# An LSTM layer with a residual: the bias by an accumulating DMA, and other amounts of work in the last 43 steps

## The chip, the cores and the metric

The kernel runs on one core of a Trainium2 chip. The metric is the device time of one execution in microseconds (us); the lower, the better. A core has five engines that work beside one another, each through its own list of instructions in order: TensorE (PE in the profile; PEld is its weight load), VectorE (DVE), ScalarE (ACT), GpSimd (POOL) and SyncE (SP). Here SP does nothing but issue DMAs; sixteen DMA engines move the data. TensorE writes into PSUM, eight banks of 128 partitions x 512 fp32 columns; everything else lives in SBUF or in DRAM.

## The reference

An LSTM layer with 512 time steps, a batch of 32 and 512 hidden units, all in fp32; its output is added to its input.

```python
xW = jnp.einsum('ntd,dg->ntg', x, Wx) + b          # (32, 512, 2048)
def step(carry, xw_t):
    prev_h, prev_c = carry
    a = xw_t + prev_h @ Wh                         # Wh: 512 x 2048
    i = jax.nn.sigmoid(a[:, :Hd]);  f = jax.nn.sigmoid(a[:, Hd:2 * Hd])
    o = jax.nn.sigmoid(a[:, 2 * Hd:3 * Hd]);  g = jnp.tanh(a[:, 3 * Hd:])
    next_c = f * prev_c + i * g
    next_h = o * jnp.tanh(next_c)
    return ((next_h, next_c), next_h)
return x + hs                                      # hs: all next_h; h0 = cond_1024, c0 = 0
```

Two matrix products of the same size are in it. The recurrent one, prev_h @ Wh, has to be done step by step. The input product x @ Wx can be done ahead for many time steps at once, and the kernel does it with a fast matrix multiplication (sums of blocks of x, sums of blocks of Wx, fewer products, and then sums of the products).

## The kernel before, in words

**Steps.** The loop `for k in range(T)` at the end of the kernel writes out 512 steps. In step k TensorE adds the recurrent product (`h_part`, L755: 16 matmuls of 384 columns and 16 of 128) onto PSUM banks that already hold xW + b for this step. They were seeded by ScalarE copies of the tile `xw[k]`: `seed_first` (L740, 384 columns, in step k-2) and `seed_last` (L746, 128 columns, in step k-1). The cell (`cell`, L792 to L800) is a chain of ScalarE and VectorE operations that ends in a transpose, L800, whose output `ht` is what the next step's matmuls wait for. `put_step` (L853) then adds the residual on Pool, and every second step SP stores two steps of output (L856) and loads two steps of residual (`load_residual`, L223).

**Windows.** Step k also carries window v = k + 4 of the input product. Steps 0 to 19 serve the head (48 time steps); from window START = 24 on come fourteen superblocks of 32 time steps each. A superblock has R = 26 products, begun in 26 of its 32 windows, and each product is seven groups of four 256-column matmuls (`product`, L465), spread over five windows by `products`. ScalarE and VectorE empty the banks in `evacuate`. VectorE's sums are kept in a list `due`, each with a window by which it has to be done and a cost in columns; `run_due(v, room)` runs what is due now, and ahead of time as much as `room` columns allow, each sum at its columns plus FIXED = 160. A window's allowance is ROOM = 4300 columns (HEAD_ROOM = 5000 in the head). At its start `evacuate` runs sums up to FIRST_SUMS = 1200 columns. The sums are L400 (blocks of x), L428 to L431 (the four inner sums, 128 x 128), L628 (half of a sum of products, 512 columns), L644 (a whole one, 1024 columns), L499 and L506 (within a product). Finished sums go to DRAM by `store` (L528, four DMAs).

**The bias.** In step k SP loads the tile `xw[k+3]`, 128 x 512 fp32, from DRAM (`load_xw`, L714), and Pool adds the bias to `xw[k+2]` in place (`add_bias`, L717). `bias_sb` is a constant 128 x 512 tile in SBUF. There are four `xw` buffers. 488 time steps take this way: the first 8 and the last 16 (the tail, t = 496 to 511) do not. Their plain products (`direct`, L670) are added to the bias by VectorE on the way from PSUM (`keep_direct`, L686).

**The order on SP.** SP issues in program order: in a step the residual load, the xw load, the stores, then `fetch` (L916: the factors wa of the product two windows on; L920: wb of this window's), then the output store.

**Half steps.** The last window of superblock products begins at LAST = 470. From step HALVES = 469 on, the cell is done in two halves of the hidden units (`h_halves`, L769, with 256-column matmuls; `cell_halves`, L814 to L840, chain ends L830), so that the next step's matmuls can begin on the first half of `ht`. In these 43 steps the free room on TensorE holds the tail's plain products: 16 time steps x NJ = 4 pieces (t, q), each of four 512-column matmuls. `tail_products(v)` takes one piece in the first window and two in each one after, until all 64 are done; that is in step 501.

Of the kernel before, what the change touches and what calls it, by code (L numbers as in the profile page):

```python
# [9 lines left out]
F32 = mybir.dt.float32  # L10
# [4 lines left out]
P = 128  # L15
B = 32
T = 512
NJ = 4
G = 4
# [3 lines left out]
C = 256  # L23
# [15 lines left out]
TAIL = 2 * ROW  # L39
NSB = (T - HEAD - TAIL) // PER  # L40
END = HEAD + NSB * PER
# [5 lines left out]
ROOM = 4300  # L47
FIRST_SUMS = 1200
BETWEEN = 1300
HEAD_ROOM = 5000  # L50
COPIED = (23, 24, 25)
SLACK = [3, 3, 5, 8]
AHEAD = 5
# [88 lines left out]
def windows_of(k):  # L142

    return [k + 4]


START = windows_of(HEAD - LEAD)[0]
# [4 lines left out]
def begin(n):  # L152

    half, at = divmod(n, R // 2)
    return PER // 2 * half + at + (at >= 5) + (at >= 9)
# [7 lines left out]
LAST = START + PER * (NSB - 1) + begin(R - 1)  # L163
HALVES = LAST + 3 - 4
# [7 lines left out]
def kernel(  # L172
# [9 lines left out]
    nc = tc.nc  # L182
# [5 lines left out]
    upool = ctx.enter_context(tc.tile_pool(name="upool", bufs=1))  # L188
# [13 lines left out]
    bias_sb = const.tile([P, G * P], F32, name="bias_sb")  # L202
# [3 lines left out]
    raw = [raw_sb[:, i] for i in range(8)]  # L206
    tt_ = [const.tile([P, 4, C], F32, name=f"t_{i}") for i in range(8)]
    rows, xw, stored = {}, {}, {}
# [11 lines left out]
    def load_residual(t):  # L220
        m = xr[t] = xr[t + 1] = opool.tile([P, 2, NJ, B], F32, name=f"xr_{t}", tag="xr")
        i, a = divmod(t, ROW)
        nc.sync.dma_start(  # L223
            out=m.rearrange("p t q b -> p (t q b)"),
            in_=x[i][:, a * P : (a + 2) * P],
        )
# [24 lines left out]
    def t_sums(i):  # L251
        w, t = raw[i], tt_[i]
        return [
            lambda: nc.vector.tensor_sub(t[:, 0::3], w[:, 1::2], w[:, 0:2]),
            lambda: nc.vector.tensor_sub(t[:, 1], w[:, 3], t[:, 0]),
            lambda: nc.vector.tensor_sub(t[:, 2], w[:, 2], t[:, 1]),
        ]
# [290 lines left out]
    for i, (_, a, b) in enumerate(C_OPS):  # L548
        n = ready[R + i]
        uses[a] += 1  # L550
        uses[b] += 1
        for v, other in ((a, b), (b, a)):
            if v < R and (v != n or other == v or n in COPIED):
                copied.add(v)
# [6 lines left out]
    for v in range(len(ready) - 1, R - 1, -1):  # L561
        n = ready[v]
        if (n in C_OPS[v - R][1:] and n not in COPIED) or any(ready[u] == n and (u in at_half) for u in users[v]):
            at_half.add(v)
# [5 lines left out]
    for v in range(len(ready) - 1, R - 1, -1):  # L570
        n = ready[v]
# [90 lines left out]
    def flat(bank):  # L662
        return bank if len(bank.shape) == 2 else bank.rearrange("p n c -> p (n c)")

    def direct(t, bank, qs=range(4)):
        i, a = divmod(t, ROW)
        for q in qs:
            k, e = divmod(q, 2)
            for j in range(NJ):
                nc.tensor.matmul(  # L670
                    flat(bank)[j * B : (j + 1) * B],
                    rows[i][:, a, q],
                    raw[NJ * k + j][:, 2 * e : 2 * e + 2].rearrange("p n c -> p (n c)"),
                    start=q == 0,
                    stop=True,
                    skip_group_check=True,
                )

    def keep_direct(t, bank, room=None):
        if room is not None:  # L680
            xw[t] = room
        elif t < 4:
            xw[t] = upool.tile([P, G * P], F32, name=f"xw_{t}", tag="xw", bufs=4)
        else:
            xw[t] = node_free[t - 4].rearrange("p t e b -> p (t e b)")
        nc.vector.tensor_add(xw[t], flat(bank), bias_sb)  # L686

    pieces = [(t, q) for t in range(END, T) for q in range(NJ)]
    whole = []
    tail_banks = [p5, accs[1 - LAST % 2], accs[LAST % 2], *pps]  # L690

    def tail_room():
        if not node_free:
            f = free.pop(0)
            node_free.extend(f[:, e].rearrange("p (t e b) -> p t e b", t=ROW, e=2) for e in range(2))
        return node_free.pop(0).rearrange("p t e b -> p (t e b)")

    def tail_products(v):
        if v < LAST + 3:
            return  # L700
        for t in whole:
            keep_direct(t, tail_banks[(t - END) % 6], tail_room())
        whole.clear()
        room = 1 if v <= LAST + 3 else 2
        for t, q in pieces[:room]:
            direct(t, tail_banks[(t - END) % 6], (q,))
            if q == NJ - 1:
                whole.append(t)
        del pieces[:room]

    def load_xw(t):
        xw[t] = upool.tile([P, G * P], F32, name=f"xw_{t}", tag="xw", bufs=4)
        i, a = divmod(t, ROW)
        nc.sync.dma_start(out=xw[t], in_=stored[i][a])  # L714

    def add_bias(t):
        nc.gpsimd.tensor_add(xw[t], xw[t], bias_sb)  # L717

# [15 lines left out]
    def seed_first(t):  # L736
        if t == HALVES:
            seed_half(t, 0)
        elif t < HALVES:
            nc.scalar.copy(gates[t % 2][:, 0:IFG], xw[t][:, 0:IFG])  # L740
# [131 lines left out]
    def prepare(v):  # L872

        job = jobs.get(v)
        ops = []
        if job is None or job.w >= START:
            return ops
        i, j = job.kind
        for k in range(2):
            if (i, k) not in head_sums:  # L880
                if (i, 0) not in head_sums:
                    both = spool.tile([P, 2, 4, 4, B], F32, name=f"s_h{i}", tag="sums", bufs=2)
                head_sums[i, k], more = inner_sums(block(raw_block(i, k)), both[:, k])
                ops += more
        job.factors = lambda s: [
            (left(block(raw_block(i, k)), s, head_sums[i, k]), raw_factor(NJ * k + j, s)) for k in range(2)
        ]
        job.finish = finish_unit(job, i, j)
        job.release = lambda: None
        return ops  # L890
# [45 lines left out]
    with tc.manual_schedule():  # L936
        warm = work.tile([P, G, P], F32, name="warm", tag="s")
        nc.scalar.activation(warm[:, 0], c_init, AF.Sigmoid)
        for m in range(3 * NJ):
            nc.tensor.matmul(  # L940
                pps[2][m % NJ * B : (m % NJ + 1) * B].rearrange("p n c -> p (n c)"),
                c_init[:, 0:B],
                c_init.unsqueeze(1).to_broadcast([P, 4, P]),
                start=True,
                stop=True,
            )
        nc.vector.transpose(
            bias_sb.rearrange("p (m l) -> p m l", l=B),
            bias_t.unsqueeze(2).to_broadcast([P, G * NJ, B]),
        )  # L950
        firsts = [gates[0], gates[1], pps[0], pps[1]]
        for q in range(4):
            for t in range(4):
                direct(t, firsts[t], (q,))
        for i in range(6):
            for op in t_sums(i):
                op()
        for op in prepare(0):
            op()
        products(0)  # L960
        for t in range(4):
            keep_direct(t, firsts[t])
        for i in range(6, 8):
            for op in t_sums(i):
                op()
        push_factors()
        for v, t in enumerate(range(4, ROW), 1):
            direct(t, gates[t % 2])
            for op in prepare(v):
                op()  # L970
            if v < 4:
                evacuate(v, 0)
            run_due(0, 2400)
            keep_direct(t, gates[t % 2])
            if v < 4:
                products(v)
                fetch(v)
        seed_first(0)
        seed_last(0)
        seed_first(1)  # L980

        for k in range(T):
            if k % 2 == 0 and k + 2 < T:
                load_residual(k + 2)
            if 2 * 4 - 3 <= k and k + 3 < END:
                load_xw(k + 3)
            (h_part if k < HALVES else h_halves)(k)
            if 2 * 4 - 2 <= k and k + 2 < END:
                add_bias(k + 2)
            for m, v in enumerate(windows_of(k)):  # L990
                if v == START + 4:
                    assert len(due) == 0 or due[0][0] >= START
                    head_done()
                announce(v)
                room = ROOM if v >= START - 4 else HEAD_ROOM
                run_due(v, room - evacuate(v, room))
                products(v)
                tail_products(v)
                fetch(v)
                if k == T - 2:  # L1000
                    x_last()
                if m == 0:
                    (cell if k < HALVES else cell_halves)(k)
                    seed_first(k + 2)
                    seed_last(k + 1)
                for op in prepare(v + 1):
                    op()
        assert not due
# [51 lines left out]
```

## Time and profile before

| | |
|---|---|
| median of 3 runs | 3136.37 us (3133.24 to 3139.02) |
| the profiled execution | 3136.89 us, span 3135.0 us, granted clock 1.00 |
| TensorE busy | 3101.0 us, 99% |
| VectorE busy | 2421.7 us, 77% |
| ScalarE busy | 1697.0 us, 54% |
| Pool busy | 1030.9 us, 33% |
| DMA queue of SP | 683.39 MB, 67.3% of 16 engines' span |

The span is the time from the first to the last instruction. A row of the timeline reads: start, duration (us), engine, line of the kernel, operation, output <- inputs, partitions x elements, number of instructions merged into the row, and in brackets how long the engine had been idle before and what released it. Ends of matmuls are modelled; their starts are the safer number. A row of a group of instructions reads: line, engine, operation, tiles, count | total busy us, mean ns of one | idle time of the engine before them and what ended most of it. A row of a DMA group ends in the size of one and the median time from issue to landing.

### The profile page before, as it was taken

To read this page: it belongs to the slowest core of one execution; us is meant where nothing else is said; L and a number is where in the kernel's file an instruction comes from. 1 tells how busy PE (TensorE), PEld (TensorE's weight loads), DVE (VectorE), ACT (ScalarE), POOL (GpSimd) and SP (SyncE) were. 2 spreads that over 40 slices of the span, in tenths; PEclk is the share of its full clock that TensorE was granted. 3 is DMA by queue.
4 is the path that set the end of the run, shared out by engine and by line. 5 is a ranking of instruction groups with operands and counts; after the bars stand their busy time and mean duration, and the time that the engine had idled before them with its cause. 6 is when DMAs were issued, how large, how long until landed. Compare 5 with 4: busy or idle time off the path is not lost.

```text
span 3135.0 us, 133350 instructions
## 1 busy us (share of the span) xinstructions
PE 3101.0 (99%) x56184; PEld 1986.8 (63%) x56184; DVE 2421.7 (77%) x6337; ACT 1697.0 (54%) x5186; POOL 1030.9 (33%) x1001
## 2 busy tenths in 40 slices
PE   9999999999999999999999999999999999999997
PEld 4665666666666666666666666666666666666565
DVE  6637787887888878788787887878888788887544
ACT  2445555555555555555555555555555555555444
POOL 0223333333333333333333333333333333333320
PEclk9999999999999999999999999999999999999999
DMA  8746776767768676676777767777686776867420
GB/s 293 246 147 212 239 241 202 265 214 248 228 207 263 219 253 212 225 253 216 251 229 230 243 223 246 224 240 241 203 269 210 243 234 208 265 215 234 142 66 25
DMA packets 341287, 691.93 MB, mean 221 GB/s; under 512 B 44752, under 2 KB 113360, under 8 KB 340176
## 3 DMA queue, kind: packets, MB, share of 16 engines
q1 hardware_dynamic: 340544, 683.39, 67.3%
q8 instruction: 442, 7.24, 1.0%
q14 instruction: 157, 1.29, 0.1%
q10 hardware_dynamic: 144, 0.01, 0.0%
HBM read 501.56 MB, written 181.67 MB: 218 GB/s over the span
## 4 chain that ended last, share of the span: by engine, by line
PE 76%; DVE 18%; ACT 3%; issue 2%; DMA 1%; DVEq 0%; SPq 0%; ACTq 0%
PE gates L755 39%; PE pp L465 13%; PE acc L465 13%; PE p L465 4%; PE gates L769 4%; DVE t L644 2%; DVE s L430 1%; DVE t L628 1%; DVE raw_sb L644 1%; DVE c L797 1%; ACT ig L798 1%; DVE ht L800 1%; DVE fc L799 1%; PE pp L670 1%; DVE s L428 1%
## 5 line engine op out<-in xcount | busy, mean ns | idle before, releaser
L755 PE MATMUL gates<-wh_sb,ht 128*32 128x384 f32 (+1 forms) x29952 | 1714.5, 380 | 12.0 <-DVE ht L800 9.5
L755 PEld LDWEIGHTS gates<-wh_sb,ht 128*32 128x32 f32 x29952 | 1026.0, 110 | 718.5 <-issue 600.8
L853 POOL TENSOR_TENSOR oc<-xr,ht 128x128 f32<-128x128 f32 x509 | 406.0, 798 | 1997.3 <-DVE ht L800 1794.7
L717 POOL TENSOR_TENSOR xw<-xw,bias_sb 128x512 f32<-128x512 f32 x488 | 640.5, 1313 | 89.9 <-DMA xw<-xw 53.4
L792 ACT ACTIVATE s<-gates 128x256 f32<-128x256 f32 x469 | 180.2, 384 | 570.0 <-PE gates L755 570.0
L465 PE MATMUL pp<-wb,nodes 128*32 128x256 f32 x3808 | 306.1, 379 | 0.0
L799 DVE TENSOR_TENSOR fc<-s,ig 128x128 f32<-128x128 f32 x469 | 138.3, 295 | 176.3 <-ACT ig L798 176.3
L504 ACT COPY pp<-pu 128x512 f32<-128x512 f32 x384 | 231.7, 603 | 60.2 <-DVE t L628 22.1
L795 DVE TENSOR_TENSOR fc<-s,c 128x128 f32<-128x128 f32 x468 | 140.8, 301 | 143.8 <-ACT s L792 141.8
L798 ACT ACTIVATE ig<-c 128x128 f32<-128x128 f32 x469 | 145.3, 310 | 165.5 <-DVE c L797 145.4
L740 ACT COPY gates<-xw 128x384 f32<-128x384 f32 x465 | 219.8, 473 | 4.8 <-DVE nodes L686 3.0
L794 ACT ACTIVATE s<-gates 128x128 f32<-128x128 f32 x469 | 130.1, 277 | 170.2 <-PE gates L755 170.2
L506 DVE TENSOR_TENSOR pp<-acc,p 128x256 f32<-128x256 f32 x384 | 162.8, 424 | 69.3 <-ACT pp L505 69.3
L465 PE MATMUL acc<-wb,s 128*32 128x256 f32 x2576 | 207.1, 380 | 1.0
L465 PE MATMUL p<-wa,s 128*32 128x256 f32 x2576 | 206.9, 379 | 0.0
L465 PE MATMUL pp<-wb,s 128*32 128x256 f32 x2576 | 206.8, 379 | 0.0
L465 PE MATMUL acc<-wa,s 128*32 128x256 f32 x2576 | 206.7, 380 | 0.0
L499 DVE TENSOR_TENSOR pu<-acc,p 128x256 f32<-128x256 f32 x384 | 159.4, 415 | 35.1 <-ACT p L496 21.9
L800 DVE STREAM_TRANSPOSE ht<-fc 128x128 f32<-128x128 f32 x469 | 146.0, 311 | 50.1 <-DVE fc L799 1.4
L505 ACT COPY pp<-acc 128x256 f32<-128x256 f32 x384 | 139.0, 362 | 77.3 <-DVE t L628 28.4
L769 PE MATMUL gates<-wh_sb,ht 128*32 128x256 f32 x2752 | 157.5, 379 | 14.7 <-DVE fc L820 14.7
L496 ACT COPY p<-p 128x256 f32<-128x256 f32 x384 | 146.4, 381 | 28.0 <-PE p L465 25.8
(218 smaller groups left out, 4637.2 us busy)
## 6 DMA issues: line engine op xcount, KB each, us to landing
wb<-keep_b SPq DMA_DIRECT2D x322, 512.0 KB, 5.5
xw<-xw SPq DMA_DIRECT2D x488, 256.0 KB, 4.2
wa<-keep_a SPq DMA_DIRECT2D x322, 384.0 KB, 4.4
xw<-t SPq DMA_DIRECT2D x348, 128.0 KB, 3.6
xw<-raw_sb SPq DMA_DIRECT2D x280, 128.0 KB, 3.1
xr<-in_x_dram SPq DMA_DIRECT2D x256, 128.0 KB, 3.1
out_dram<-oc SPq DMA_DIRECT2D x255, 128.0 KB, 2.6
row<-in_x_dram SPq DMA_DIRECT2D x63, 512.0 KB, 6.7
```

Of the source, the lines that this page charges most:

```text
L465: nc.tensor.matmul(dst[t * B : (t + 1) * B], a[:, t], w, start=s in (1, 5) and m == 0, stop=True, skip_group_check=True,)
L504: nc.scalar.copy(job.pp[0], job.pu)
L506: nc.vector.tensor_add(job.pp[1][:, 1], job.acc, job.p5)
L717: nc.gpsimd.tensor_add(xw[t], xw[t], bias_sb)
L740: nc.scalar.copy(gates[t % 2][:, 0:IFG], xw[t][:, 0:IFG])
L755: nc.tensor.matmul(g[j * B : (j + 1) * B, cols], state["ht"][:, k, :], wh_sb[:, k, j, cols], start=False, stop=True, skip_group_check=True,)
L769: nc.tensor.matmul(bank_half(m)[j * B : (j + 1) * B], state["ht"][:, k, :], half(wh_sb[:, k, j], m), start=False, stop=True, skip_group_ch ...
L792: nc.scalar.activation(s[:, 0:2], g[:, 0:2], AF.Sigmoid)
L798: nc.scalar.activation(tc_t, c, AF.Tanh)
L799: nc.vector.tensor_mul(h, s[:, 3], tc_t)
L800: nc.vector.transpose(ht.rearrange("p q b -> p (q b)"), h)
L853: (nc.gpsimd if t < T - 3 else nc.vector).tensor_add(state["oc"][:, tt % 2], xr[t][:, tt % 2], ht)
```

## The change

Four things change.

1. The bias. SP first fills the tile `xw[k+4]` with the bias by a DMA from `bias_sb` to SBUF (`fill_bias`, in step k). In the next step a DMA from DRAM, issued on Pool's queue, adds the stored product onto it (`load_xw(k+3)`, with `accum_op` add). Pool's addition is gone.
2. From step HALVES - 1 = 468 on a window's allowance for sums is HALF_ROOM = 1500 columns, not 4300. FIRST_SUMS stays at 1200.
3. The tail's pieces are cut: the first piece of a time step (q = 0) still has 512 columns, the other three are two of 256 each.
4. `tail_products(v)` takes pieces until the columns taken so far reach 512 x 4 x (v - 472) x 16 / 41, about 799 columns for each window from 473 on; the last is done in window 513, step 509.

```diff
+HALF_ROOM = 1500
...
-    def direct(t, bank, qs=range(4)):
+    def direct(t, bank, qs=range(4), cols=slice(0, 512)):
...
-                    flat(bank)[j * B : (j + 1) * B],
+                    flat(bank)[j * B : (j + 1) * B, cols],
                     rows[i][:, a, q],
-                    raw[NJ * k + j][:, 2 * e : 2 * e + 2].rearrange("p n c -> p (n c)"),
+                    raw[NJ * k + j][:, 2 * e : 2 * e + 2].rearrange("p n c -> p (n c)")[:, cols],
...
-    pieces = [(t, q) for t in range(END, T) for q in range(NJ)]
-    whole = []
+    pieces = [(t, q, e) for t in range(END, T) for q in range(NJ) for e in ((slice(0, 512),) if q == 0 else (slice(0, C), slice(C, 512)))]
+    whole, tail_columns = [], [0]
...
-        room = 1 if v <= LAST + 3 else 2
-        for t, q in pieces[:room]:
-            direct(t, tail_banks[(t - END) % 6], (q,))
-            if q == NJ - 1:
+        columns = 512 * NJ * (v - LAST - 2) * TAIL // (T - 1 - LAST)
+        while pieces and tail_columns[0] < columns:
+            t, q, cols = pieces.pop(0)
+            direct(t, tail_banks[(t - END) % 6], (q,), cols)
+            tail_columns[0] += cols.stop - cols.start
+            if q == NJ - 1 and cols.stop == 512:
                 whole.append(t)
-        del pieces[:room]
+
+    def fill_bias(t):
+        xw[t] = upool.tile([P, G * P], F32, name=f"xw_{t}", tag="xw", bufs=4)
+        nc.sync.dma_start(out=xw[t], in_=bias_sb)
 
     def load_xw(t):
-        xw[t] = upool.tile([P, G * P], F32, name=f"xw_{t}", tag="xw", bufs=4)
         i, a = divmod(t, ROW)
-        nc.sync.dma_start(out=xw[t], in_=stored[i][a])
-
-    def add_bias(t):
-        nc.gpsimd.tensor_add(xw[t], xw[t], bias_sb)
+        nc.gpsimd.dma_start(out=xw[t], in_=stored[i][a], accum_op=mybir.AluOpType.add)
...
+            if 2 * 4 - 4 <= k and k + 4 < END:
+                fill_bias(k + 4)
             if 2 * 4 - 3 <= k and k + 3 < END:
                 load_xw(k + 3)
             (h_part if k < HALVES else h_halves)(k)
-            if 2 * 4 - 2 <= k and k + 2 < END:
-                add_bias(k + 2)
...
-                room = ROOM if v >= START - 4 else HEAD_ROOM
+                room = HEAD_ROOM if v < START - 4 else ROOM if k < HALVES - 1 else HALF_ROOM
                 run_due(v, room - evacuate(v, room))
```

## The prediction

> **What bounds the kernel now.** I read the page first, then the table of windows, then the timeline of two stages.
>
> ```profile
> PE 3101.0 (99%) x56184; PEld 1986.8 (63%) x56184; DVE 2421.7 (77%) x6337; ACT 1697.0 (54%) x5186; POOL 1030.9 (33%) x1001
> PE 76%; DVE 18%; ACT 3%; issue 2%; DMA 1%; DVEq 0%; SPq 0%; ACTq 0%
> 0.00:100.00 100.00, 98.63 (x1500) 49.76 (x1504) 65.97 (x145) 30.27 (x83) 5.78 (x11) 1.00 0.79 278
> 1200.00:1600.00 400.00, 398.10 (x7303) 257.74 (x7296) 330.53 (x833) 227.15 (x675) 141.74 (x134) 1.00 0.71 232
> ```
>
> TensorE is busy for 99% of the span (the windows' last three numbers are granted clock, DMA share and GB/s: 1.00, 0.71, 232 in the main stage). Yet the chain that ended last runs through VectorE for 18%, so there are places where TensorE waits for it. Ends of matmuls are modelled, so I measure the loss by starts, over one superblock of 32 steps:
>
> ```profile
> 1502.49 3.66 PE L755 MATMUL gates<-wh_sb,ht 128*32 128x384 f32 x64
> 1508.53 3.66 PE L755 MATMUL gates<-wh_sb,ht 128*32 128x384 f32 x64
> ```
>
> ```profile
> 1412.73 3.66 PE L755 MATMUL gates<-wh_sb,ht 128*32 128x384 f32 x64 [0.25 <-DVE ht L800]
> ...
> 1597.78 3.66 PE L755 MATMUL gates<-wh_sb,ht 128*32 128x384 f32 x64
> 1601.22 0.64 PE L465 MATMUL pp<-wb,row 128*32 128x256 f32 x8
> ...
> 1603.38 0.64 PE L465 MATMUL pp<-wb,s 128*32 128x256 f32 x8
> 1604.28 0.81 PE L755 MATMUL gates<-wh_sb,ht 128*32 128x384 f32 x5 [0.25 <-DVE ht L800]
> ```
>
> The first two rows are the starts of an undisturbed step: 6.04 us. It holds the recurrent product h_part and six groups of products; from 1601.22 to 1603.38 lie five groups, 0.432 us each, so h_part takes 6.04 - 2.59 = 3.45. The superblock took 1604.28 - 1412.73 = 191.55 us. Its 26 products of seven groups are 182 groups, ten under six a step: 32 x 6.04 - 10 x 0.432 = 188.96 us of work. So 2.6 us per superblock, 36 us in fourteen, is waiting. The last of these steps shows for what:
>
> ```profile
> 1599.02 1.27 POOL L717 TENSOR_TENSOR xw<-xw,bias_sb 128x512 f32<-128x512 f32 x1
> 1599.22 1.23 DVE L431 TENSOR_TENSOR s<-nodes,s 128x128 f32<-128x128 f32 x1
> ...
> 1600.37 0.28 DVE L429 TENSOR_TENSOR s<-s,nodes 128x128 f32<-128x128 f32 x1
> ...
> 1600.62 0.38 ACT L792 ACTIVATE s<-gates 128x256 f32<-128x256 f32 x1 [1.01 <-PE gates L755]
> ...
> 1602.24 0.28 DVE L795 TENSOR_TENSOR fc<-s,c 128x128 f32<-128x128 f32 x1
> ...
> 1603.82 0.31 DVE L800 STREAM_TRANSPOSE ht<-fc 128x128 f32<-128x128 f32 x1
> ```
>
> L431 on 128x128 takes 1.23 us while Pool adds the bias (L717), where its twin L429 takes 0.28 behind it: VectorE lost 0.95 us. The cell's first product L795 could start when the sigmoid ends (1600.62 + 0.38 = 1601.00) and starts at 1602.24, 1.24 late; ht follows, and the step from 1597.78 to 1604.28 lasts 6.50 us where its work is 6.04. A lateness of 1.24 cost 0.46, so up to 0.78 is free. Another kind, one superblock later:
>
> ```profile
> 1640.43 1.28 POOL L717 TENSOR_TENSOR xw<-xw,bias_sb 128x512 f32<-128x512 f32 x1
> 1640.78 1.47 DVE L628 TENSOR_TENSOR raw_sb<-t,t 128x512 f32<-128x512 f32 x1
> 1642.18 0.68 DVE L628 TENSOR_TENSOR raw_sb<-raw_sb,pp 128x512 f32<-128x512 f32 x1
> ...
> 1643.12 0.64 PE L465 MATMUL pp<-wb,nodes 128*32 128x256 f32 x8
> 1643.38 0.41 DVE L499 TENSOR_TENSOR pu<-acc,p 128x256 f32<-128x256 f32 x1
> ...
> 1643.84 0.64 PE L465 MATMUL acc<-wb,s 128*32 128x256 f32 x8
> ```
>
> Again a two-tile sum beside L717 (1.47 against 0.68, 0.79 lost); L499 comes late, and the acc group, due at 1643.12 + 0.43 = 1643.55, starts at 1643.84.
>
> **The bias, main stage.** Removed: 488 Pool additions, and 488 loads on SP. Added: 488 fills on SP, one step earlier in program order (t = k+4 in place of k+3), and 488 accumulating DMAs on Pool's queue.
>
> ```profile
> L717 POOL TENSOR_TENSOR xw<-xw,bias_sb 128x512 f32<-128x512 f32 x488 | 640.5, 1313 | 89.9 <-DMA xw<-xw 53.4
> xw<-xw SPq DMA_DIRECT2D x488, 256.0 KB, 4.2
> q1 hardware_dynamic: 340544, 683.39, 67.3%
> ```
>
> Pool is off the path (33% busy), so its 640.5 us are worth nothing in themselves. What they give back is VectorE's lost time. In the step above, 0.95 of 1.24 us goes, and 0.29 is under the free 0.78: the 0.46 vanishes. In the second case the 0.79 us more than cover the 0.29. The cost of the Pool issue to VectorE the trace does not show, as no DMA is issued from Pool. One end is nothing (it reads no tile, where L717 reads two); the other end is L717's own, about 1 us again, and then nothing is won. Longer than L717 it could be too, a loss that I leave to the slower cases. I take the lower end, since the delayed rows are all additions beside an addition, and four fifths of the 36 us, 29, because some of the waits will have another cause behind the first. The Trainium skill, page "SBUF — State Buffer", section "Who interferes with whom", says that a VectorE tensor_tensor with two SBUF inputs contends with a GpSimd instruction that reads SBUF, not with one that only writes it. The trace agrees on the reading half (1.23 against 0.28); no row shows the writing half, by which a descriptor writer would free VectorE wholly, and the time would fall by the full 36.
>
> Two waits are added. First on SP:
>
> ```profile
> 1506.82 0.54 SPq L714 DMA_DIRECT2D xw<-xw  x1
> ...
> 1507.32 0.27 ACT L746 COPY gates<-xw 128x128 f32<-128x128 f32 x1
> ...
> 1507.45 0.46 SPq L916 DMA_DIRECT2D wa<-keep_a  x1
> ...
> 1508.51 1.28 POOL L717 TENSOR_TENSOR xw<-xw,bias_sb 128x512 f32<-128x512 f32 x1
> ...
> 1512.86 0.47 ACT L740 COPY gates<-xw 128x384 f32<-128x384 f32 x1
> ```
>
> In a step without a residual load SP reaches the load's place at 1506.82. The fill stands there and must wait for the last reader of the same buffer, the seed copy L746, done at 1507.59: some 0.8 us, and behind it stand the stores and the fetches of wa and wb. The wa at 1507.45 is for the job two steps on, so 0.8 us is hidden. Pool then waits for the fill's landing: issue 1507.6 + 4.2 = 1511.8, while Pool's turn (the place of L717, one step on) is 1508.51 + 6.04 = 1514.55; nothing. From there the tile must be whole when L740 copies it. The step of these rows begins at 1508.53; its fill is accumulated one step later and seeded two steps later, so at 1512.86 + 2 x 6.04 = 1524.9: 10.4 us for issue and landing, against 4.2 for the load it replaces. Six microseconds of cover; gone, each further microsecond would cost one per step. Pool's oc addition is queued behind this DMA and is needed only after the next ht.
>
> **DMA traffic.** The fill adds 256 KB per step to the 232 GB/s x 5.99 us = 1389 KB moved now; accumulating adds between nothing and the reading and writing of further tiles. The engines have shown 278 GB/s at a share of 0.79, so 352 at full use. With m tile-times for an accumulation in place of one for a load, a step needs (1389 + 262 m) / 352 us: 4.7 at m = 1, 5.4 at 2, 6.2 at 3, against 5.9 of TensorE work. Nearest row is the plain load, and an addition must read its target as well: I take 2, hidden. The Trainium skill, page "DMA: Bandwidth & Descriptors", section "Rules for kernel authors", says that an accumulate reads its destination and writes it later; that is m = 2, and by it the sum stands.
>
> **The half steps.** From step 469 on each step is h_halves, then some of the tail's plain products.
>
> ```profile
> 2907.19 3.66 PE L769 MATMUL gates<-wh_sb,ht 128*32 128x256 f32 x64
> ...
> 2910.32 0.23 ACT L816 ACTIVATE s<-gates 128x64 f32<-128x64 f32 x1
> ...
> 2911.02 1.23 DVE L644 TENSOR_TENSOR t<-t,raw_sb 128x1024 f32<-128x1024 f32 x1
> ...
> 2912.16 0.22 DVE L820 TENSOR_TENSOR fc<-s,c 128x64 f32<-128x64 f32 x1
> ...
> 2927.84 3.66 PE L769 MATMUL gates<-wh_sb,ht 128*32 128x256 f32 x64 [1.08 <-DVE fc L820]
> ...
> 2993.33 0.63 PE L670 MATMUL acc<-raw_sb,row 128*32 128x512 f32 x2
> ...
> 2995.05 3.66 PE L769 MATMUL gates<-wh_sb,ht 128*32 128x256 f32 x64
> ...
> 3077.77 3.66 PE L769 MATMUL gates<-wh_sb,ht 128*32 128x256 f32 x64
> ...
> 3126.25 3.66 PE L769 MATMUL gates<-wh_sb,ht 128*32 128x256 f32 x64 [1.20 <-DVE fc L820]
> ```
>
> From 2907.19 to 3126.25 are 42 steps, 219.06 us. The 29 from 2927.84 to 3077.77 take 5.17 each: 3.45 + 1.72 for two pieces of 512 columns (2993.33 to 2995.05). The ten after 3077.77 take 4.85 each with next to no products: there the cell's chain is the limit, and TensorE idles 1.4 us. The first three (20.65 us) are late by VectorE: in the first, sums up to 2911.02 + 1.23 hold L820 to 2912.16, though the gates were ready at 2910.55. The new rule gives 2048 x 16 / 41 = 799 columns per step in units of 256 or 512. Counted through, steps 472 to 510 get 1024 columns eight times and 768 or fewer 31 times; 768 columns need 3.45 + 1.29 = 4.74, under the chain's 4.85. So 8 x 5.17 + 31 x 4.85 = 191.7, where 149.93 + 48.48 = 198.4 stood. The first three: with room for 1500 columns one sum of 1024 runs per step (the first allowance of 1200 lets it), 1.2 us, which fits between the second transpose and the next L820. Then products bound them: 3.45 + 3 x 0.43 (jobs) + 1.72 = 6.46, 3.45 + 0.43 + 1.29 = 5.17, and 4.85, in all 16.5 in place of 20.65. Splitting pieces doubles the weight loads of three in four, hidden as in the groups of 256 columns, which pass at 0.43. The stage gains 6.7 + 4.1 = 10.8 us. If the sums' due times force them together, up to 4 of it is lost.
>
> **Sum.** Profiled execution 3136.9 us (span 3135.0; the median of the runs is 0.5 lower): 3136.9 - 29 - 10.8 = 3097.
>
> **Rivals.** (1) The main stage isn't relieved: issuing from Pool holds VectorE up as L717 did. For it: it starts at the same moment, right behind the oc addition. Against: it reads no tiles. Only the tail gains: 3136.9 - 10.8 = 3126. (2) Slower: the DMA engines become the bound. For it: a share of 0.71 before two more tile-times. Against: 278 GB/s were reached. It decides from m = 2.8 on, where a step needs 6.0 us; at m = 3 it needs 6.18, 0.19 over today's 5.99, x 485 steps = 92, less 10.8: 3218. (3) The change doesn't do what it says in the half steps, the sums being forced by their due times: 3136.9 - 29 - 6.7 = 3101. (4) Gains and new waits cancel: within 0.2% (6.3 us, about what a measurement of this kernel can tell from no change).
>
> **Chances.** Both gains, 3088 to 3108: 0.57 (rival 3 in it with 0.1); tail alone or a partly relieved main stage, 3108 to 3130: 0.17; cancelled 0.05; slower 0.21, nearly all rival 2. Faster is 0.57 + 0.17 = 0.74. The low end is 36 + 10.8 off, 3090, and 2 for the first rows' rounding: 3088; the high end takes in rival 1 and the cancelled case, 3142. The likeliest case alone has 3088 to 3108.
>
> **What would show it.** L431, L430 and L429 on 128x128 fall to 0.28 us throughout; Pool's busy time falls by 640; superblocks take 189 to 190 us (191.55 now); half steps alternate between 4.85 and 5.17; no step after 469 has more than one or two L644. Wrong would be: sums still of 1.2 us near Pool's issue (rival 1); a DMA share near 1.0, landings of wb well over 5.5 us and TensorE waiting for wa, wb or L740 (rival 2).

## The result, and the profile after

| | before | after |
|---|---|---|
| median | 3135.66 us (3130.67 to 3139.02, 22 runs) | 3139.64 us (3128.97 to 3151.96, 22 runs) |
| ratio | | 1.0017 [1.0008, 1.0025] |
| profiled execution | 3136.89 us, span 3135.0 | 3151.96 us, span 3150.2 |

The change leaves the time about where it was, slower by 0.17%: 3140 us where 3097 was forecast. The profiled execution of after is at the slow end of its own runs, 12 us over their median, so the stage sums below show some 11 us more loss than the medians have. Lines of the kernel after are one to two higher than before (L757 is `h_part`, L771 `h_halves`, L466 the products, L719 the accumulating DMA, L715 the fill, L742 the first seed, L802 the transpose).

The page after, its totals, the DMA queues and the chain that ended last:

```profile
PE 3101.8 (98%) x56568; PEld 2007.1 (64%) x56568; DVE 2241.6 (71%) x6337; ACT 1704.8 (54%) x5186; POOL 824.3 (26%) x1001
q0 software_dynamic: 70272, 127.96, 24.8%
PE 88%; DMA 9%; ACT 1%; DVE 1%; issue 1%; SPq 0%; POOL 0%; POOLq 0%; DVEq 0%; ACTq 0%
wb<-keep_b SPq DMA_DIRECT2D x322, 512.0 KB, 6.8
xw<-bias_sb SPq DMA_DIRECT2D x488, 256.0 KB, 5.8
xw<-xw POOLq DMA_DIRECT2D x488, 256.0 KB, 6.2
```

VectorE's 18% of the chain has become 1%, and its busy time fell by 180 us: what the change was forecast to win was won. In its place DMA stands with 9%. The factors wb land after 6.8 us (5.5 before) and the stored product after 6.2 (4.2 before).

Two stages tell how much, by starts of matmuls in the timeline. After: step 0, the first half step and the last.

```profile
47.40 3.64 PE L757 MATMUL gates<-wh_sb,h_init 128*32 128x384 f32 x64
...
2933.16 3.66 PE L771 MATMUL gates<-wh_sb,ht 128*32 128x256 f32 x64 [0.85 <-ACT raw_sb L617]
...
3141.50 3.66 PE L771 MATMUL gates<-wh_sb,ht 128*32 128x256 f32 x64 [1.17 <-DVE fc L822]
```

Before, step 0 (its half steps begin at 2907.19 and the last at 3126.25, shown above):

```profile
47.19 3.64 PE L755 MATMUL gates<-wh_sb,h_init 128*32 128x384 f32 x64
```

The steps ahead of the half steps, "main" from here on, took 2933.16 - 47.40 = 2885.76 us against 2860.00: 25.8 longer. The half steps took 208.34 against 219.06: 10.7 shorter, where 208.2 was forecast. So all that went wrong lies in main. The windows of after, first the same long one as before and then one stretch in windows of a step (columns: busy time of PE, PEld, DVE, ACT and POOL, then granted clock, DMA share, GB/s):

```profile
1200.00:1600.00 400.00, 395.97 (x7336) 262.52 (x7332) 302.56 (x836) 227.49 (x674) 112.52 (x134) 1.00 0.96 279
...
1705.00:1711.00 6.00, 6.00 (x120) 3.98 (x113) 5.26 (x15) 3.37 (x11) 1.62 (x2) 1.00 0.88 236
...
1717.00:1723.00 6.00, 6.00 (x117) 3.98 (x113) 3.67 (x12) 4.07 (x13) 1.34 (x2) 1.00 0.99 241
1723.00:1729.00 6.00, 6.00 (x116) 4.00 (x112) 3.79 (x12) 2.84 (x9) 1.06 (x2) 1.00 1.02 369
...
1741.00:1748.00 7.00, 6.27 (x116) 3.40 (x112) 5.32 (x16) 3.07 (x11) 0.53 (x2) 1.00 0.97 272
1748.00:1754.00 6.00, 3.95 (x76) 2.00 (x67) 4.93 (x14) 2.52 (x8) 2.37 (x2) 1.00 0.99 236
1754.00:1760.00 6.00, 5.00 (x57) 2.60 (x61) 1.09 (x3) 1.62 (x4) 1.65 (x3) 0.72 1.05 397
1760.00:1766.00 6.00, 6.00 (x116) 3.53 (x112) 5.06 (x14) 3.11 (x9) 2.65 (x3) 1.00 0.73 181
```

The same place before:

```profile
1704.00:1710.00 6.00, 6.00 (x117) 3.97 (x113) 4.94 (x15) 2.88 (x10) 2.07 (x2) 1.00 0.43 140
...
1716.00:1722.00 6.00, 6.00 (x119) 3.99 (x112) 3.56 (x12) 3.32 (x11) 1.71 (x2) 1.00 0.98 336
1722.00:1728.00 6.00, 6.00 (x120) 3.96 (x115) 4.30 (x14) 3.38 (x11) 1.75 (x2) 1.00 1.03 380
1728.00:1734.00 6.00, 6.00 (x120) 3.96 (x116) 4.75 (x14) 3.83 (x12) 2.06 (x2) 1.00 0.59 195
```

This stretch holds the row loads: once in a superblock, in four steps on end, SP also fetches 512 KB of x per step (`load_row`). Before, these steps already filled the DMA engines (0.98, 1.03), and the steps beside them left room to catch up (0.43, 0.59; two fuller ones, 0.88 and 0.98, follow before the next with 0.63 and 0.44). After, the steps ahead and behind stand at 0.87 to 1.05 too, up to 1760 (0.73), the backlog stays, and 7 to 26 us after the issue of the last of these loads TensorE loses 0.73, 2.05 and 1.00 us in three windows on end. The timeline of after shows the way:

```profile
1719.37 0.62 SPq L214 DMA_DIRECT2D row<-in_x_dram  x1
...
1728.72 0.47 SPq L715 DMA_DIRECT2D xw<-bias_sb  x1
...
1733.66 0.48 SPq L214 DMA_DIRECT2D row<-in_x_dram  x1
...
1734.39 0.31 DVE L802 STREAM_TRANSPOSE ht<-fc 128x128 f32<-128x128 f32 x1
...
1736.39 0.88 POOL L719 DMA_DIRECT2D xw<-xw  x1 [6.62 <-ACT gates L742]
...
1736.99 0.77 POOL L855 TENSOR_TENSOR oc<-xr,ht 128x128 f32<-128x128 f32 x1
...
1737.79 0.34 SPq L858 DMA_DIRECT2D out_dram<-oc  x1
...
1744.42 0.48 ACT L742 COPY gates<-xw 128x384 f32<-128x384 f32 x1 [3.57 <-DMA xw<-xw]
1744.76 2.94 SPq L529 DMA_DIRECT2D xw<-slot_h  x4
...
1745.26 1.08 PE L757 MATMUL gates<-wh_sb,ht 128*32 128x128 f32 x32 [0.73 <-ACT gates L748]
...
1748.23 0.44 SPq L922 DMA_DIRECT2D wb<-keep_b  x1
...
1755.00 1.08 PE L466 MATMUL acc<-wb,s 128*32 128x256 f32 x8 [3.05 <-DMA wb<-keep_b]
```

Two transfers come late. The accumulation issued at 1736.39 lands 8.0 us later, the seed copy L742 has waited 3.57 us for it, and `h_part` stops for 0.73. Then wb comes, and TensorE stands for 3.05. This wb landed 6.6 us after its issue, no longer than the median wb of after; it was late because it was issued late, at 1748.23. The rows between show a coupling of the queues that leads there. Pool idles 6.62 us before it can issue the accumulation of 1736.39, since the fill that it adds onto, issued at 1728.72, took 7.0 us to land. (The row names L742 as the releaser; releasers are inferred, and by the order of the issues it is this fill.) The oc addition stands behind it on Pool and starts 2.3 us after its ht is there (1734.70), and SP's output store, with the next fill, stores and fetches behind it, follows only at 1737.79.

SP is held up in a second way. Its transfers carry eight semaphores in turn, and in this trace none of the 2788 is issued before the one eight places ahead of it has landed. So late landings delay SP's later issues: the row load of 1733.66 took 11.0 us to land, and the store of 1744.76 goes out right behind it. By an estimate from the landings in the traces, such waits took SP 41 us before and 136 us after.

### The profile page after: what moved, and what is told of

It is laid out like the page before. It is cut to its first block, busy times and chain, and to the rows that moved or that the text cites. A ratio compares the mean times of both kernels' runs of the same rounds, so it can differ in the third digit from the quotient of the medians.

```text
span 3150.2 us, 134152 instructions
## 1 busy us (share of the span) xinstructions
PE 3101.8 (98%) x56568; PEld 2007.1 (64%) x56568; DVE 2241.6 (71%) x6337; ACT 1704.8 (54%) x5186; POOL 824.3 (26%) x1001
## 3 DMA queue, kind: packets, MB, share of 16 engines
q1 hardware_dynamic: 340544, 683.39, 64.1%
q0 software_dynamic: 70272, 127.96, 24.8%
## 4 chain that ended last, share of the span: by engine, by line
PE 88%; DMA 9%; ACT 1%; DVE 1%; issue 1%; SPq 0%; POOL 0%; POOLq 0%; DVEq 0%; ACTq 0%
PE gates L757 45%; PE pp L466 15%; PE acc L466 15%; PE p L466 5%; PE gates L771 5%; DMA xw<-xw 3%; DMA wb<-keep_b 3%; DMA xw<-bias_sb 2%; PE pp L671 1%; PE gates L671 1%; PE acc L671 1%; PE p L671 0%; ACT gates L742 0%; DMA xw<-slot_h 0%; DMA xw<-slot 0%
## 5 line engine op out<-in xcount | busy, mean ns | idle before, releaser
L757 PE MATMUL gates<-wh_sb,ht 128*32 128x384 f32 (+1 forms) x29952 | 1719.5, 380 | 4.0 <-DVE ht L802 2.6
L757 PEld LDWEIGHTS gates<-wh_sb,ht 128*32 128x32 f32 x29952 | 1034.9, 110 | 694.0 <-issue 595.1
L719 POOL DMA_DIRECT2D xw<-xw x488 | 432.3, 886 | 824.7 <-DMA xw<-bias_sb 231.3
L466 PE MATMUL pp<-wb,nodes 128*32 128x256 f32 x3808 | 311.7, 383 | 0.0
L742 ACT COPY gates<-xw 128x384 f32<-128x384 f32 x465 | 220.7, 475 | 108.4 <-DMA xw<-xw 104.7
L466 PE MATMUL acc<-wb,s 128*32 128x256 f32 x2576 | 209.4, 382 | 34.5 <-DMA wb<-keep_b 33.3
L466 PE MATMUL acc<-wa,s 128*32 128x256 f32 x2576 | 211.0, 384 | 0.0
L466 PE MATMUL pp<-wb,s 128*32 128x256 f32 x2576 | 210.6, 383 | 0.0
L466 PE MATMUL p<-wa,s 128*32 128x256 f32 x2576 | 207.8, 379 | 0.0
L802 DVE STREAM_TRANSPOSE ht<-fc 128x128 f32<-128x128 f32 x469 | 146.0, 311 | 49.7 <-DVE fc L801 0.9
L493 ACT COPY pu<-acc 128x256 f32<-128x256 f32 x384 | 143.1, 373 | 50.2 <-PE acc L466 50.2
```

The costliest lines, as they stand in the source:

```text
L466: nc.tensor.matmul(dst[t * B : (t + 1) * B], a[:, t], w, start=s in (1, 5) and m == 0, stop=True, skip_group_check=True,)
L719: nc.gpsimd.dma_start(out=xw[t], in_=stored[i][a], accum_op=mybir.AluOpType.add)
L757: nc.tensor.matmul(g[j * B : (j + 1) * B, cols], state["ht"][:, k, :], wh_sb[:, k, j, cols], start=False, stop=True, skip_group_check=True,)
L802: nc.vector.transpose(ht.rearrange("p q b -> p (q b)"), h)
```

## The experiments

Two theories. **T1, the DMA engines' time:** the fill and the accumulation take so much of it that the bursts of row loads can no longer be caught up. **T2, the order of the waits:** fill, accumulation and seed are a chain over SP's and Pool's queues, and holding these queues up makes the other transfers late, whatever the traffic. Times of main and of the half steps are differences of starts, as above.

**Each half of the change alone.** The tail alone, with Pool's addition kept:

```diff
+HALF_ROOM = 1500
...
-    pieces = [(t, q) for t in range(END, T) for q in range(NJ)]
+    pieces = [(t, q, e) for t in range(END, T) for q in range(NJ) for e in ((slice(0, 512),) if q == 0 else (slice(0, C), slice(C, 512)))]
...
+        columns = 512 * NJ * (v - LAST - 2) * TAIL // (T - 1 - LAST)
...
+                room = HEAD_ROOM if v < START - 4 else ROOM if k < HALVES - 1 else HALF_ROOM
```

> The kernel before with the two edits to the half steps alone (HALF_ROOM, and the tail's pieces in 256 columns spread by the column rule); the bias stays with Pool. Theory T1 (the half steps gain what was forecast, and the main stage loses it again by DMA traffic): half steps take 208.3 us in place of 219.1, the main stage is unchanged, so 3136 - 10.7 = 3125 us, ratio 0.9966. Rival: if the gain in the half steps needed the freed Pool, less than 5 us, 3131 or more.

The bias alone:

```diff
...
-        nc.sync.dma_start(out=xw[t], in_=stored[i][a])
+        nc.gpsimd.dma_start(out=xw[t], in_=stored[i][a], accum_op=mybir.AluOpType.add)
...
+            if 2 * 4 - 4 <= k and k + 4 < END:
+                fill_bias(k + 4)
...
-            if 2 * 4 - 2 <= k and k + 2 < END:
-                add_bias(k + 2)
```

> The kernel before with the bias by the filled tile and the accumulating DMA alone; half steps as before. T1: the main stage alone carries the loss, so 3139.6 + 10.7 = 3150 us, ratio 1.0046, with stalls of 2 to 6 us once per superblock, a few steps after the row loads. Rival (the two parts get in each other's way, and the bias alone would gain): under 3136 us.

The tail alone: 3126.97 us, 0.9976 [0.9967, 0.9985], 7.2 below before. Its half steps took 211.51, not 208.3. The timeline of the tail alone shows what the other 3 us hang on:

```profile
2924.47 3.66 PE L771 MATMUL gates<-wh_sb,ht 128*32 128x256 f32 x64
...
2925.73 1.39 POOL L855 TENSOR_TENSOR oc<-xr,ht 128x128 f32<-128x128 f32 x1 [2.81 <-DVE ht L832]
...
2927.09 1.28 POOL L719 TENSOR_TENSOR xw<-xw,bias_sb 128x512 f32<-128x512 f32 x1
...
2927.63 0.82 DVE L822 TENSOR_TENSOR fc<-s,c 128x64 f32<-128x64 f32 x1 [0.22 <-ACT s L816]
...
2929.89 3.66 PE L771 MATMUL gates<-wh_sb,ht 128*32 128x256 f32 x64 [0.47 <-DVE fc L822]
```

L822, 0.22 us when undisturbed (L820 before), takes 0.82 beside Pool's bias addition, and the step lasts 5.42, where it lasts 4.83 in after. Pool's addition lies there because oc, ahead of it, took 1.39 us beside a sum of 1024 columns (L645), 0.46 in the step of before that begins at 2933.01. The bias alone: 3147.41, 1.0048 [1.0032, 1.0063], 13.3 above before. So the loss is the bias's, and 13.3 - 7.2 = 6.1 is near the 4 of both together.

**What the addition on Pool had cost.** Before, without `add_bias`:

```diff
             (h_part if k < HALVES else h_halves)(k)
-            if 2 * 4 - 2 <= k and k + 2 < END:
-                add_bias(k + 2)
```

> The kernel before with Pool's bias addition left out, so the bias is missing from the time steps 8 to 495; nothing else is changed. Theory of the forecast (beside L717, VectorE's sums with two SBUF inputs take a microsecond more, and that makes 36 us of TensorE waits in the main stage): 3136 - 36 = 3100 us, give or take 5, ratio 0.9885; the sums L428 to L431 take 0.28 us throughout. Rival (the waits have other causes, the long sums only lie beside them): 3125 or more.

It took 3099.6 us, 0.9891 [0.9878, 0.9903]. Timeline of this kernel:

```profile
47.42 3.66 PE L755 MATMUL gates<-wh_sb,h_init 128*32 128x384 f32 x64
...
2873.28 3.66 PE L769 MATMUL gates<-wh_sb,ht 128*32 128x256 f32 x64
```

Main takes 2825.86 us, 34.1 less than before. That is the whole price of Pool's bias addition. Here L431, the sum of 1.23 us, takes 279 ns on average (463 before), which fits the delayed sums as the way; no run parts them from the addition's other effects.

**The fill on another engine.** The change, but ScalarE copies the bias into the tile, just ahead of the cell, and SP issues no fill:

```diff
     def fill_bias(t):
-        nc.sync.dma_start(out=xw[t], in_=bias_sb)
+        nc.scalar.copy(xw[t], bias_sb)
...
-            if 2 * 4 - 4 <= k and k + 4 < END:
-                fill_bias(k + 4)
...
+                if 2 * 4 - 4 <= k and k + 4 < END:
+                    fill_bias(k + 4)
                 if m == 0:
                     (cell if k < HALVES else cell_halves)(k)
```

> The changed kernel, but the tile is filled with the bias by a ScalarE copy just ahead of the cell, not by a DMA. T1 (the DMA engines are too near their limit): a fill's packets are some 12% of the engines' time, the share falls from 0.95 to about 0.83, the stalls once per superblock go, VectorE stays relieved: 3136 - 36 - 10.7 = 3090 us, give or take 8, ratio 0.985. T2 (the stalls come from the order of waits between SP, Pool and the four tile buffers): the fill's wait leaves SP as well, so this run alone doesn't part T1 and T2. Rival: ScalarE's 0.6 us more per step delays the cell and costs the gain: 3110 or more.

It took 3091.95 us (3091.17 to 3093.38), 0.9867 [0.9854, 0.9879]: faster than both kernels. Its copies as a group, the long window and the timeline:

```profile
L715 ACT COPY xw<-bias_sb 128x512 f32<-128x512 f32 x488 | 308.2, 632 | 0.0
...
1200.00:1600.00 400.00, 400.00 (x7408) 265.48 (x7404) 305.54 (x847) 266.35 (x751) 113.25 (x136) 1.00 0.86 236
...
47.14 3.67 PE L757 MATMUL gates<-wh_sb,h_init 128*32 128x384 f32 x64
...
2873.00 3.66 PE L771 MATMUL gates<-wh_sb,ht 128*32 128x256 f32 x64
...
3080.75 3.66 PE L771 MATMUL gates<-wh_sb,ht 128*32 128x256 f32 x64 [1.17 <-DVE fc L822]
```

Main is again 2825.86, the half steps are 207.75, and TensorE never stops in the long window, at a DMA share of 0.86. The accumulation itself, on Pool's queue as in the change, costs nothing here. wb lands after 6.3 us in the median, not much less than in after, and TensorE never waits for it: what made it late in after was its issue. The copies' 308.2 us lie in ScalarE's idle time. Against it, main of after is 59.9 us longer in its profiled execution; by the medians the whole is 47.7 longer.

But this kernel takes away both the traffic of the fill (T1) and its waits on SP (T2). So the traffic alone was put back into it, as a store of the same 256 KB from `bias_sb` to a DRAM buffer that nobody reads:

```diff
+            if 2 * 4 - 4 <= k and k + 4 < END:
+                unread = dram.tile([P, G * P], F32, name=f"unread_{k}", tag="unread", bufs=8)
+                nc.sync.dma_start(out=unread, in_=bias_sb)
```

> The run with the ScalarE fill (3092 us), with one more DMA on SP where the fill stood: 256 KB from the bias tile to a DRAM buffer that nobody reads, once per step. The traffic of the fill is back, and none of its waits. T1 (the DMA engines' time is the cause): share back to 0.95 or more, landings of wb and of the accumulation grow, stalls once per superblock return, 3120 to 3160 us. T2 (the fill's place in the order of waits is the cause): 3092, give or take 4.

It took 3129.21 us (3119.9 to 3138.61), 0.9986 [0.9977, 0.9995]. Its long window, its chief new wait (total, times, longest) and one wait of SP's queue:

```profile
1200.00:1600.00 400.00, 394.98 (x7268) 258.02 (x7263) 299.47 (x828) 260.73 (x735) 110.87 (x133) 0.99 0.95 276
PE acc L466 <- DMA wb<-keep_b: 24.3, 11, 4.9
...
SPq L858 <- DMA unread<-bias_sb: 15.8, 17, 1.9
```

37 of the 48 us are lost again, and nothing here leads from a fill to Pool and the seeds: the traffic is enough, as T1 says. But the store does bring waits back, which the expectation left out: SP's later issues wait for its landing in their turn of the eight semaphores (259 us of such waits on all landings by the same estimate, 46 in the run without the store). So the run does not part the traffic from every wait on SP. The other 10 can be the rest of the queues' coupling, or the other target of the store; no run tells these apart.

**The accumulation without adding.** The change, the DMA on Pool's queue a plain load:

```diff
-        nc.gpsimd.dma_start(out=xw[t], in_=stored[i][a], accum_op=mybir.AluOpType.add)
+        nc.gpsimd.dma_start(out=xw[t], in_=stored[i][a])
```

> The changed kernel with a plain load on Pool's queue in place of the accumulating one; it overwrites the filled tile, so the bias is missing from the time steps 8 to 495. The order of waits is the same. T1: the accumulation's 24.8% of the engines' time falls to about 12%, the share from 0.95 to 0.83, the stalls go, 3090 us, give or take 6. T2: 3130 or more.

It took 3093.72 us, 0.9869 [0.9856, 0.9881]. Its queue and long window:

```profile
q0 software_dynamic: 39040, 127.96, 14.5%
...
1200.00:1600.00 400.00, 400.00 (x7429) 265.15 (x7424) 305.92 (x846) 230.66 (x683) 91.18 (x135) 1.00 0.85 280
```

Every wait of fill, Pool and seed is still in the program, and the loss is gone: the order of the waits costs nothing by itself, and T2 falls as the main cause. By the timeline of after, the waits are the way by which full DMA engines reach TensorE. This run moves the bytes of after (280 GB/s, 279) at a share of 0.85 in place of 0.96. Bytes don't say how loaded the engines are; the share does. The 127.96 MB took 24.8% of 3150.2 us when added and 14.5% of 3092.8 when not: 781 against 448 us, 1.7 times.

**The burst.** The change, with the row loads as eight halves in eight steps, begun four steps earlier:

```diff
-        sb, rest = divmod(v + 8 - START, PER)
+        sb, rest = divmod(v + 12 - START, PER)
...
-        if rest < MO and 0 <= sb < NSB:
-            load_row(HEAD // ROW + MO * sb + ROWS_AT[rest])
+        if rest < 2 * MO and 0 <= sb < NSB:
+            load_row(HEAD // ROW + MO * sb + ROWS_AT[rest // 2], ROW // 2 * (rest % 2), ROW // 2 * (rest % 2) + ROW // 2)
```

> The changed kernel with the four row loads of a superblock (512 KB each, in four steps running) cut into eight halves over eight steps, begun four windows earlier. The total traffic is the same. T1, with the burst of row loads on a share of 0.95 as the cause of the backlog: the stalls shrink by half or more, 3100 to 3125 us. Rival under T1 (the average load alone is too high, wherever the rows stand): 3135 or more, stalls at other places. T2: 3140 as before.

It took 3110.01 us, 0.9926 [0.9913, 0.9939]. Its long window:

```profile
1200.00:1600.00 400.00, 399.32 (x7382) 264.12 (x7377) 305.46 (x844) 230.12 (x681) 113.69 (x135) 1.00 0.97 279
```

The same bytes at the same share, spread over twice the steps, and 30 of the 48 us are gone. So the loss isn't the average share alone, it is the average and the burst. The edit also begins the loads earlier; how much of the 30 us that gives, no run tells.

**The fill on a third queue.** The change, the fill issued from ScalarE:

```diff
-        nc.sync.dma_start(out=xw[t], in_=bias_sb)
+        nc.scalar.dma_start(out=xw[t], in_=bias_sb)
```

> The changed kernel, with the fill DMA issued on ScalarE's queue, not SP's: the same traffic, but SP's fetches no longer stand behind the fill's wait for the last reader of the tile. T1: 3140 us, give or take 8, stalls as before. T2: the stalls go, 3095 to 3110.

It took 3197.35 us (3175.87 to 3205.82), 1.0194 [1.017, 1.0218], a miss for both theories. Two groups by line show the waits (the last number is the idle time that the named releaser ended), and a row of SP's waits. With the third queue:

```profile
L466 PE MATMUL acc<-wb,s 128*32 128x256 f32 x2576 | 209.6, 386 | 64.8 <-DMA wb<-keep_b 61.4
L742 ACT COPY gates<-xw 128x384 f32<-128x384 f32 x465 | 219.9, 473 | 11.5 <-DMA xw<-xw 8.4
...
SPq L922 <- DMA xw<-bias_sb: 78.1, 34, 7.0
```

After:

```profile
L466 PE MATMUL acc<-wb,s 128*32 128x256 f32 x2576 | 209.4, 382 | 34.5 <-DMA wb<-keep_b 33.3
L742 ACT COPY gates<-xw 128x384 f32<-128x384 f32 x465 | 220.7, 475 | 108.4 <-DMA xw<-xw 104.7
```

Taken off SP, the fill no longer makes the seeds late (8.4 us, 104.7 in after), but wb, on which TensorE itself waits, is later (61.4, 33.3), and the time is 58 us longer. The edit did not free SP of the fill. In this trace ScalarE's DMAs carry the same eight semaphores as SP's, so an issue on SP also waits until a fill of ScalarE's has landed: 78.1 us ahead of the fetch of wb (L922), where after has no such wait. So the run does not test T2 as it was meant to. Its traffic is that of after, at a share of 0.94, so the traffic alone does not set the loss. That these waits are what costs the 58 us is argued from the rows; whether a third queue also takes turns from SP's, no run shows.

## Why the prediction was right or wrong

**VectorE's relief: right, sized 5 us low.** Where the fill is not a DMA, main gains all of it, 34.1 us (29 was taken, of 36). The sums that stood at 1.23 us beside Pool's addition are undisturbed, by the groups of after:

```profile
L432 DVE TENSOR_TENSOR s<-nodes,s 128x128 f32<-128x128 f32 x252 | 71.1, 282 | 0.0
```

That is L431 of before, at the forecast 0.28 us. **The Pool issue** was put at nothing to VectorE, with L717's price as the other end: right. This is the half of the rule that no row of before showed (the Trainium skill, page "SBUF — State Buffer", section "Who interferes with whom"): a GpSimd instruction that only writes SBUF doesn't contend with a tensor_tensor of two SBUF inputs. The trace agrees, if an issue only writes, which no row shows: 282 ns with 488 issues of 886 ns on Pool, and of all the sums L432 those that lie beside an issue take 288 ns on average, the others 280. Rival 1 is out. For Pool itself the issues were left out of the forecast: they take 432 us, so its busy time fell by 206.6 (1030.9 to 824.3), not 640; nothing hung on it.

**The half steps: right.** 208.34 us, forecast 208.2. The parts fit too: 17.1 us for the first three steps (16.5 forecast, and 16.5 with ScalarE filling) and 191.2 for the rest (191.7). Not foreseen: 3 of the 10.7 need the addition on Pool to be gone, which else runs beside the cell's products.

**The two waits: wrong by what else was full.** The "six microseconds of cover" were counted with a landing of 4.2 us. The accumulation's became 6.2, the fill's 5.8, with Pool waiting between the two, and the seeds L742 waited 104.7 us in all. That oc "is queued behind this DMA and is needed only after the next ht" left out that SP's output store waits for oc, and all of SP behind it; that SP has only eight transfers in flight was not in the sum either. The seeds themselves stop TensorE for little (0.73 us above); 33.3 us of its waits in after end with wb, in 14 waits. Those wb landed 5.7 to 8.7 us after their issue, beside a median of 6.8 over all, so what stands out is their issue, as in the timeline above.

**DMA traffic: the step that failed.** "I take 2, hidden": the 2 was near. One plain load of these bytes at the mean rate of SP's queue before is 127.96 / 683.39 x 67.3% x 3135.0 = 395 us; the accumulations took 781, m = 2.0; against plain loads on the same queue it is 1.7. The average was near too: 5.4 of 5.9 us is 0.92, measured 0.96. "Hidden" was wrong, because it was judged on the average step. The steps of the row loads were full before the change; what hid their excess was the room beside them, and the change took that. Rival 2 had the mechanism, and its signs came: a share of 0.96, landings of wb at 6.8 us, TensorE waiting for wb and for L742 (L740 before). But its point of decision (m = 2.8, where the average step is full) was set by the same average: it came at 2.0 and cost 48 us, not 92. Without the fill's DMA the forecast holds: 3092 with ScalarE filling, 3097 forecast.

**The sum.** 34.1 + 10.7 = 44.8 us won, about 48 lost: rival 4's case of gains and new waits that cancel, given a chance of 0.05. A faster kernel was given 0.74, and the time did not fall. That 3140 lies inside the range of 3088 to 3142, by its upper end, is luck: the loss, which the sum put at nothing, happened to be of the size of the gains.

## What to carry to other kernels

Judge new DMA traffic on the fullest stretch, not on the mean: take windows of one step over a whole period, and ask whether the steps beside the burst can still catch up. Look also at what a queue waits for before it can issue: a transfer can be late though it lands in its usual time. An accumulating DMA cost 1.7 to 2.0 times a plain load of its size here, and a fill by DMA comes on top; where a compute engine has idle time, a copy there (632 ns on ScalarE) was free and takes the load off the DMA engines. Before paying for traffic, try to spread the burst that it collides with.

## What the runs showed of the hardware, not expected

A stall of TensorE costs more than its length. After the one of 3.05 us the groups come at twice their pitch (0.43 us), by the timeline of after:

```profile
1755.83 1.11 PE L466 MATMUL acc<-wa,row 128*32 128x256 f32 x8
1756.68 1.11 PE L466 MATMUL acc<-wa,s 128*32 128x256 f32 x8
```

They start 0.83 and 0.85 us behind the group before them, and the granted clock of the window from 1754 is 0.72. Over after's span it is 0.995 (1.000 before), which is, as an estimate, 0.005 x 3150 = 16 us of lost clock in this execution. The Trainium skill, page "TensorE: Matmul & The Clock Gate", section "Part 1: The HAM clock gate", says that the array goes to half its clock after an idle window of about 3.4 us. The trace agrees with the halving; here stalls of 3.05 us and, at 982, of 2.29 us were enough (the granted clock is 0.50 from 983.3 to 986.7), while one of 2.8 us that ended at 1561 was not (1.00 behind it).

The DMA engines also gave 280 GB/s at a share of 0.85 for plain transfers, and 279 at 0.96 with the accumulations.
